# A two-layer graph network: the first mixer's sum of keys by values taken in node order in the head, and the second layer's loop with TensorE, VectorE and ScalarE in a written-out order

## The chip, the cores and the metric

The kernel runs on one core of one Trainium2 chip. A core has TensorE (PE, matrix products and transposes), VectorE (DVE), ScalarE (ACT), GpSimd (POOL, which issues the indirect DMAs here) and SyncE (SP, which issues plain DMAs). The metric is the device time of the whole program in microseconds (us); the profile is one execution recorded by the hardware profiler.

## The reference

There are 3125 nodes with 256 features and 53,125 edges (every random edge both ways, and a loop on each node). Two layers follow one another; each adds message passing, a mixer and a feed-forward part to the residual `x`.

```python
xn = _layernorm(x)
x = x + gnn0(xn, src, dst, edge_weight) + mix0(xn[None])[0]
x = x + ffn0(_layernorm(x)[None])[0]                      # 32 experts, argmax
xn = _layernorm(x)
x = x + gnn1(xn, edge_index, edge_type_64) + mix1(xn[None])[0]
x = x + ffn1(_layernorm(x)[None], edge_index)[0]          # 4 experts, routed by graph attention
```

The first mixer is attention without a softmax. Its `kv` and the norm of each column of `k2` are sums over all nodes, so the order of the nodes does not matter to them:

```python
q, k, v = split(x @ W_qkv + b_qkv)
q2 = (q - mean(q))**2 ; k2 = (k - mean(k))**2
k2 = l2_normalize_over_nodes(k2 / (sum(k2) + eps)) ; q2 = l2_normalize_over_features(q2 / (sum(q2) + eps))
kv = einsum('bnc,bnd->bcd', k2, v)
out = (v + einsum('bnc,bcd->bnd', q2, kv) / sqrt(N)) @ W_out + b_out
```

The second layer's message passing is an attention over the edges of each node, with four heads of 64:

```python
mod_k = K[src] + 0.2 * rel_w[edge_relations][:, None, :]
scores = einsum('ehd,ehd->eh', Q[dst], mod_k) / 8
w = segment_softmax(scores, dst)
msgs = segment_sum(w[:, :, None] * V[src], dst)
out = layernorm(msgs @ Wo + bo + xn) * gamma + beta
```

## The kernel before

Nodes are sorted by degree and put into 25 tiles (`NT`) of 128. Tile `t` has `SLOTS[t]` edge slots a node: 38 in the first tile, 25 in the second, falling to 10 in the last, 444 in all. One indirect DMA of POOL gathers one slot's rows for 128 nodes.

**The head** (`prepare`) counts degrees, sorts the nodes (`ordered`), makes a flag that says whether the fast path holds, and normalizes the 25 tiles of nodes in their given order; SP stores these rows to a table `xtab` in memory. When the head is done, all engines read the flag and branch.

**The front** (`front`) gathers the residual rows in sorted order into `self.xs`, and runs the first mixer (`first_mixer`): for each tile a layernorm (`normed`), a transpose, the products for queries, for keys and values, and for values times output weights (`products`), squares with their statistics (`squares`), and the sum `kvT` of keys by values (`sums`). The generator `counted` (from `sources`), which makes lists of edges, is advanced by one piece at every second tile. Then come a column norm `cn` and a product of `kv` with the output weights, `kvo`. After the mixer follow the first layer's message passing (gathers `g`, added up in `acc` on DVE), the experts, the products of the second layer, and the scatters that build the table `kvtab` of its keys and values.

**The second layer's loop** goes over the tiles. For each tile, `scores` gathers keys and values of up to four slots into one buffer `kv` (14 buffers), adds relation rows `pr`, multiplies by the query `q` and reduces, for each group of four slots; a softmax over the slots follows. `values` scales the value half of each buffer by the softmax weights (ACT, four instructions a slot; DVE takes one slot in eight) and adds them up on PE into `pu` through an identity matrix. `project` makes the output product `pz`. The relation rows come from a one-hot matrix: a transpose of types (`typT`), a product with selectors (`pT`), a comparison on DVE (`ohT`), a product with the relation table (`pr`). For each part of five tiles (the last two parts have three and two), `norms` finishes the second layernorm, and `router_rows` computes the rows of the router table, which POOL scatters to `htab`.

The order of the instructions on each engine is made by a scheduler that follows data and buffers; the routed stage behind the loop is the only one whose order on ACT and DVE is written by hand (`tc.manual_schedule`). The code of the loop asks for the next tile's preparations (`ready`) before the values of this one, and projects the last tile after that:

```python
sc, groups = scores(t, *this)
if t + 1 < NT:
    this = ready(t + 1)
now = t, xq, values(t, xq, sc, groups)
...
project(last[0], last[1], last[2], z[:, i, :], mv[:, i, :])
if last[0] == part[-1]:
    norms(part, z, mv)
    router_rows(part)
```

Behind the loop, the routed stage gathers from `htab` for the 4-expert feed-forward part.

Of the kernel before, what the change touches and what calls it, by code (L numbers as in the profile page):

```python
# [21 lines left out]
P = 128  # L22
N = 3125
D = 256
# [872 lines left out]
class Fast(Net):  # L897
# [32 lines left out]
    def prepare(self, ctx):  # L930
# [11 lines left out]
        flag = keep.tile([1, 1], I32, name="flag")  # L942
        self.ones3 = keep.tile([3, P], BF16, name="ones3")
# [5 lines left out]
        with ExitStack() as ctx:  # L949
# [92 lines left out]
            for t in range(NT):  # L1042
                xn = work.tile([P, D], F32, name="xn")
                self.layernorm(work, self.xs[:, t, :], xn)
                nc.sync.dma_start(self.xtab[t * P:(t + 1) * P, :], xn)
# [280 lines left out]
    def types_by_slot(self, pool, ps, t):  # L1326

        nc = self.nc
        S2 = SLOTS[t] + SLOTS[t] % 2
        pt = ps.tile([S2, P], F32, name="pT")  # L1330
        nc.tensor.transpose(pt, self.typs[t], self.ident)
        typT = pool.tile([S2, P], BF16, name="typT")
        nc.vector.tensor_copy(typT, pt)
        return typT

    def relation_one_hots(self, pool, ps, t, typT, g):

        nc = self.nc
        n = min(8, SLOTS[t] + SLOTS[t] % 2 - g)
        pt = ps.tile([P, 4, P], F32, name="pT")  # L1340
        for i in range(n // 2):
            nc.tensor.matmul(pt[:, i], self.sel[:typT.shape[0], g + 2 * i:g + 2 * i + 2, :].rearrange("s i r -> s (i r)"),
                             typT, start=True, stop=True)
        ohT = pool.tile([P, 4, P], BF16, name="ohT", bufs=3)
        nc.vector.tensor_scalar(ohT[:, :n // 2], pt[:, :n // 2], self.mod, None, op0=OP.is_equal)  # L1345
        return ohT
# [40 lines left out]
    def first_mixer(self, ctx, q2T, nq, kvo, counted):  # L1387
# [5 lines left out]
        w_kv = self.load_kb(big, "w_kv", a["mix0_wkv"])  # L1393
# [3 lines left out]
        b_qkv = self.load_terms(big, big, "b_qkv", a["mix0_b"])  # L1397
# [7 lines left out]
        for c in range(KB):  # L1405
            pw = ps.tile([P, D], F32, name="pqv", bufs=2)
            self.mm_rows(pw, w_vT[:, :, c * P:(c + 1) * P], w_o)
            nc.scalar.copy(w_vo[:, c, :], pw)
# [4 lines left out]
        pw = ps.tile([P, D], F32, name="pqv", bufs=2)  # L1413
# [4 lines left out]
        kvT = ps.tile([P, KB, D], F32, name="kvT")  # L1418
        sqs = big.tile([P, D], F32, name="sqs")
        nc.vector.memset(sqs, 0.0)  # L1420
# [5 lines left out]
        def products(t, xn):  # L1426
            xT = work.tile([P, KB, P], F32, name="xT", bufs=2)
            self.transpose_to(ps, xn, xT)
            pqv = ps.tile([P, 2, D], F32, name="pqv", bufs=2)
            pkv = ps.tile([P, 2 * D], F32, name="pkv", bufs=2)  # L1430
            self.mm_rows(pqv[:, 0], xT, w_q, b_qkv[:, 0:D])
            self.mm_rows(pkv, xT, w_kv, b_qkv[:, D:])
            self.mm_rows(pqv[:, 1], xT, w_vo, b_vo)
            return pqv, pkv

        def squares(t, pqv, pkv):

            pq = pqv[:, 0]
            st = work.tile([P, 2, 6], F32, name="mx_st")
            mv = work.tile([P, 2, 2], F32, name="mx_mv")  # L1440
            nc.vector.bn_stats(st[:, 0, :], pq)
            nc.vector.bn_stats(st[:, 1, :], pkv[:, 0:D])
            for k in range(2):
                nc.vector.bn_aggr(mv[:, k, :], st[:, k, :])
            sd = work.tile([P, 3, 2], F32, name="mx_sd")
            nc.scalar.activation(sd[:, 0, :], mv[:, :, 1], AF.Sqrt, bias=self.eps[:, 1:2],
                                 scale=float(D))
            nc.vector.reciprocal(sd[:, 1, :], sd[:, 0, :])
            nc.vector.scalar_tensor_tensor(sd[:, 2, :], mv[:, :, 0], -1.0, sd[:, 1, :],
                                           op0=OP.mult, op1=OP.mult)  # L1450
            q2 = work.tile([P, D], F32, name="q2")
            k2 = work.tile([P, D], F32, name="k2")
            v = work.tile([P, D], F32, name="v")
            sq = work.tile([P, 2, D], F32, name="sq", bufs=2)
            nc.scalar.activation(q2, pq, AF.Square, bias=sd[:, 2, 0:1], scale=sd[:, 1, 0:1])
            nc.scalar.activation(k2, pkv[:, 0:D], AF.Square, bias=sd[:, 2, 1:2],
                                 scale=sd[:, 1, 1:2])
            nc.scalar.copy(v, pkv[:, D:])
            nc.vector.tensor_add(self.xs[:, t, :], self.xs[:, t, :], pqv[:, 1])
            nc.scalar.activation(sq[:, 0, :], q2, AF.Square, accum_out=nq[:, t:t + 1])  # L1460
            nc.scalar.activation(sq[:, 1, :], k2, AF.Square)
            return q2, k2, v, sq

        def sums(t, q2, k2, v, sq):
            r = rows(t)
            self.transpose_to(ps, q2, q2T[:, :, t * P:(t + 1) * P])
            for k in range(KB):
                nc.tensor.matmul(kvT[:, k, :], v[:r, k * P:(k + 1) * P], k2[:r, :],
                                 start=(t == 0 and k == 0), stop=(t == NT - 1 and k == KB - 1))
            nc.vector.tensor_add(sqs[:r], sqs[:r], sq[:r, 1, :])  # L1470
# [3 lines left out]
        for t in range(NT + 1):  # L1474
            now = None
            if t < NT:
# [3 lines left out]
                now = t, *squares(t, *made)  # L1480
            if last:
                sums(*last)
# [4 lines left out]
        kv = big.tile([P, KB, D], F32, name="kv")  # L1487
        for k in range(KB):
            nc.vector.tensor_copy(kv[:, k, :], kvT[:, k, :])
        cn = work.tile([1, D], F32, name="cn")  # L1490
        csum = ps.tile([1, D], F32, name="pqv", bufs=2)
        nc.tensor.matmul(csum, self.ones[:, 0:1], sqs, start=True, stop=True)
        nc.scalar.activation(cn, csum, AF.Sqrt)
        nc.vector.tensor_scalar_max(cn, cn, 1e-12)
        nc.vector.reciprocal(cn, cn)
        pc = ps.tile([P, KB], F32, name="pqv", bufs=2)
        for k in range(KB):
            nc.tensor.matmul(pc[:, k:k + 1], cn[:, k * P:(k + 1) * P], self.ones[0:1, 0:1],
                             start=True, stop=True)
        rc = work.tile([P, KB], F32, name="rc")  # L1500
        nc.vector.tensor_copy(rc, pc)
        for c in range(KB):
            pw = ps.tile([P, D], F32, name="pqv", bufs=2)
            self.mm_rows(pw, kv[:, :, c * P:(c + 1) * P], w_o)
            nc.vector.tensor_scalar(kvo[:, c, :], pw, rc[:, c:c + 1], None, op0=OP.mult)
# [5 lines left out]
    def front(self, q2T, qT, kvtab, own):  # L1511
# [5 lines left out]
        with ExitStack() as ctx:  # L1517
# [4 lines left out]
            kvo = big.tile([P, KB, D], F32, name="kvo")  # L1522
# [8 lines left out]
            with ExitStack() as mctx:  # L1531
                self.first_mixer(mctx, q2T, nq, kvo, counted)
# [236 lines left out]
    def layers(self):  # L1769
# [7 lines left out]
        with ExitStack() as octx:  # L1777
# [40 lines left out]
            with tc.tile_pool(name="l1_edge", bufs=2, reuse_waits="tile") as ep, \  # L1818
                    tc.tile_pool(name="l1_ps3", bufs=1, space=PSUM, reuse_waits="tile") as ps:
                self.selectors(keep)  # L1820

                def ready(t):

                    xq = ep.tile([P, 2 * D], F32, name="xq", bufs=3)
                    nc.sync.dma_start(xq, own[t * P:(t + 1) * P, :])
                    q = ps.tile([P, D], F32, name="q", bufs=2)
                    nc.scalar.copy(q, xq[:, :D])
                    typT = self.types_by_slot(ep, ps, t)
                    return xq, q, typT, self.relation_one_hots(ep, ps, t, typT, 0)

                def scores(t, xq, q, typT, ohT):
                    S = SLOTS[t]
                    sc = ep.tile([P, S0, 4], F32, name="sc", bufs=3)
                    groups = []
                    for g in range(0, S, 4):
                        n = min(4, S - g)
                        if g % 8 == 0:
                            rr = self.relation_rows(ps, t, ohT, g)
                            if g + 8 < S:
                                ohT = self.relation_one_hots(ep, ps, t, typT, g + 8)  # L1840
                        r0 = g % 8
                        kv = ep.tile([P, 4, 2 * D], F32, name="kv", bufs=14)
# [11 lines left out]
                        nc.vector.tensor_reduce(sc[:, g:g + n, :], k4, axis=AX.X, op=OP.add)  # L1854

# [7 lines left out]
                    nc.scalar.activation(sc[:, :S], sc[:, :S], AF.Exp)  # L1863
                    nc.vector.tensor_reduce(m[:, 0, :], s4, axis=AX.X, op=OP.add)
# [3 lines left out]
                    return sc, groups  # L1868

                def values(t, xq, sc, groups):  # L1870

                    pu = ps.tile([P, D], F32, name="pu", bufs=2)
                    for g, n, kv in groups:
                        for j in range(n):
# [9 lines left out]
                            nc.tensor.matmul(pu, self.ident, v, start=(s == 0), stop=(s == SLOTS[t] - 1))  # L1884
                    return pu

                def project(t, xq, pu, z, mv):
                    u = ep.tile([P, D], F32, name="u")
                    nc.scalar.copy(u, pu)
                    uT = ep.tile([P, KB, P], F32, name="uT")  # L1890
                    self.transpose_to(ps, u, uT)
# [457 lines left out]
```

## Time and profile before

| | us |
|---|---|
| median of 3 runs | 3276.42 (3270.76 to 3286.6) |
| the profiled execution, own time | 3264.12 |
| its span | 3262.3 |
| head, until the flag is made (L1039) | 98 |
| first mixer's loop | 165 to 366 |
| rest of the mixer | 366 to 387 |
| first layer's messages, experts, tables | to 1638 |
| second layer's loop, first gather of `kvtab` to last scatter to `htab` | 1638 to 2601 |
| routed stage | to 3262 |

The profile names a group of instructions by line, engine, operation and tile, with its busy time, the mean time of one, and what ended the idle time of its engine before it ("<-"). An engine's idle time costs something only where the engine is on the path that sets the end. The granted clock (PEclk) is the share of full speed at which TensorE was let run; its mean over the span is 0.761.

### The profile page before, as it was taken

The page shows a single profiled execution, that of the slowest core. Times are in us where ns is not written, and L with a number is a line of the kernel's source. Part 1 is how long each engine was busy: PE and PEld are TensorE (multiplying, and loading weights), DVE is VectorE, ACT ScalarE, POOL GpSimd, SP SyncE. Part 2 cuts the span into 40 slices and gives each one's busy share as a digit, 9 for nine tenths or more (in the row PEclk, how much of TensorE's full clock was granted, in tenths as well). Part 3 has the DMA queues.
Part 4 walks back from the last instruction along what each step waited for, and adds up shares of the span by engine and source line. Part 5 has one row for each costly group of instructions (what it writes and reads, how often), then busy time and mean ns, then how long its engine had stood idle before and what let it go on. Part 6 is the DMA issues. An engine that isn't in the chain of part 4 may idle for free. (4 is left out here: it accounts for less than half of the span.)

```text
span 3262.3 us, 25577 instructions
## 1 busy us (share of the span) xinstructions
PE 1896.8 (58%) x7318; PEld 1140.2 (35%) x7318; DVE 1393.8 (43%) x4055; ACT 872.6 (27%) x2625; POOL 1569.9 (48%) x1675
## 2 busy tenths in 40 slices
PE   0298543556677997415415455665555543867568
PEld 0155222333344554203213343343333322444346
DVE  6487553445444341001237465765655501111026
ACT  0044200111121221001105453655443401312132
POOL 3523466546444216673764664545442074355543
PEclk9899666778788998657757676776776666888789
DMA  4312423223222210000064564545442110000001
GB/s 126 112 60 82 139 83 90 88 83 106 76 84 76 68 42 7 17 4 10 20 194 127 140 179 120 166 127 168 127 127 85 54 32 5 16 7 12 12 7 41
DMA packets 121377, 254.53 MB, mean 78 GB/s; under 512 B 36594, under 2 KB 61926, under 8 KB 120972
## 3 DMA queue, kind: packets, MB, share of 16 engines
q0 software_dynamic: 82656, 196.67, 21.8%
q1 hardware_dynamic: 30316, 47.90, 4.4%
q10 hardware_dynamic: 8256, 8.23, 0.8%
q8 instruction: 61, 1.00, 0.1%
q14 instruction: 88, 0.72, 0.1%
HBM read 228.93 MB, written 23.76 MB: 77 GB/s over the span
## 5 line engine op out<-in xcount | busy, mean ns | idle before, releaser
L1370 POOL DMA_INDIRECT g<-xtab,src x444 | 440.1, 991 | 474.4 <-DVE acc L1376 171.7
L1845 POOL DMA_INDIRECT kv<-kvtab,src x444 | 423.1, 953 | 348.5 <-ACT kv L1882 194.2
L1882 ACT ACTIVATE kv<-kv,sc 128x64 f32<-128x64 f32 x1548 | 380.0, 334 | 78.2 <-issue 48.2
L2056 POOL DMA_INDIRECT ed<-htab,nb x279 | 264.1, 947 | 274.3 <-issue 177.6
L1884 PE MATMUL pu<-kv,ident 128*128 128x256 f32 x888 | 300.6, 469 | 51.2 <-ACT kv L1882 32.1
L1647 PE MATMUL po<-w,h 128*128 128x256 f32 x800 | 230.6, 426 | 131.6 <-ACT h L1633 72.6
L1233 POOL DMA_INDIRECT gl<-gsrc,sidx x256 | 248.9, 972 | 106.9 <-issue 77.3
L2195 PE MATMUL po<-w,h 128*128 128x256 f32 x800 | 208.2, 403 | 87.0 <-issue 86.5
L2183 PE MATMUL ph<-xT,w 128*128 128x512 f32 (+1 forms) x448 | 204.0, 607 | 65.3 <-ACT h L2185 37.4
L1884 PEld LDWEIGHTS pu<-kv,ident 128*128 128x128 f32 x888 | 177.4, 225 | 129.6 <-ACT kv L1882 77.5
L1627 PE MATMUL ph<-xT,w 128*128 128x512 f32 (+1 forms) x448 | 213.7, 594 | 7.3 <-issue 3.6
L1376 DVE SCALAR_TENSOR_TENSOR acc<-g,wt,acc 128x256 f32<-128x256 f32 x419 | 194.8, 477 | 49.0 <-DMA g<-xtab,src 40.5
L1647 PEld LDWEIGHTS po<-w,h 128*128 128x128 f32 x800 | 153.0, 207 | 168.9 <-issue 77.0
L2195 PEld LDWEIGHTS po<-w,h 128*128 128x128 f32 x800 | 155.6, 199 | 136.1 <-issue 118.6
L1633 ACT ACTIVATE h<-ph,b 128x512 f32<-128x512 f32 (+1 forms) x112 | 71.7, 641 | 449.6 <-remote 194.0
L1851 DVE TENSOR_TENSOR kv<-kv,pr 128x1024 f32<-128x1024 f32 (+3 forms) x121 | 133.1, 1123 | 122.9 <-remote 82.3
L1356 PE MATMUL pr<-self.relb,ohT 128*128 128x128 bf16 x687 | 88.5, 289 | 107.3 <-DVE ohT L1345 61.4
L2183 PEld LDWEIGHTS ph<-xT,w 128*128 128x128 f32 x448 | 87.2, 209 | 167.2 <-issue 120.6
L1853 DVE TENSOR_TENSOR kv<-kv,q 128x1024 f32<-128x1024 f32 (+3 forms) x121 | 132.7, 1123 | 0.0
L1854 DVE TENSOR_REDUCE sc<-kv 128x16 f32<-128x1024 f32 (+3 forms) x121 | 132.5, 1121 | 0.1
L2185 ACT ACTIVATE h<-ph,b 128x512 f32<-128x512 f32 (+1 forms) x112 | 68.9, 641 | 229.7 <-PE ph L2183 120.1
L2074 DVE TENSOR_TENSOR ed<-ed 128x288 f32<-128x288 f32 (+12 forms) x16 | 7.5, 466 | 280.7 <-ACT ed L2072 280.7
(437 smaller groups left out, 2985.5 us busy)
## 6 DMA issues: line engine op xcount, KB each, us to landing
dr<-in_gat_dst_row SPq DMA_DIRECT2D x32, 512.0 KB
g<-xtab,src POOLq DMA_INDIRECT x444
kv<-kvtab,src POOLq DMA_INDIRECT x444
own<-xq SPq DMA_DIRECT2D x25, 256.0 KB
xq<-own SPq DMA_DIRECT2D x25, 256.0 KB
ed<-htab,nb POOLq DMA_INDIRECT x279
w<-in_ex_w ACTq DMA_DIRECT2D x2, 2048.0 KB
gl<-gsrc,sidx POOLq DMA_INDIRECT x256
```

The lines of the kernel that those rows point to most:

```text
L1233: ins = nc.gpsimd.indirect_dma_start(out=self.gl[:, :], out_offset=bass.IndirectOffsetOnAxis(ap=self.sidx2[:, c:c + 1], axis=0), in_=self. ...
L1370: nc.gpsimd.indirect_dma_start(out=g[:, s % 4, :], out_offset=None, in_=self.xtab[:, :], in_offset=bass.IndirectOffsetOnAxis(ap=self.srcs[ ...
L1376: nc.vector.scalar_tensor_tensor(acc, g[:, s % 4, :], self.wts[t][:, s:s + 1], acc, op0=OP.mult, op1=OP.add)
L1627: nc.tensor.matmul(ph[:, :n], w1[:, k, mc], xT[:, k, :n], start=(k == 0), stop=False)
L1647: nc.tensor.matmul(pos[j // 2][:, j % 2], this[:, j * P:(j + 1) * P], w2[:, m, :], start=False, stop=(m == M - 1 and (j % 2 == 1 or j == w ...
L1845: nc.gpsimd.indirect_dma_start(out=kv[:, j, :], out_offset=None, in_=kvtab[:, :], in_offset=bass.IndirectOffsetOnAxis(ap=self.srcs[t][:, g ...
L1851: nc.vector.tensor_tensor(k4, k4, rr[:, r0:r0 + n].unsqueeze(2).to_broadcast([P, n, 4, HD]), op=OP.add)
L1882: nc.scalar.activation(v[:, h * HD:(h + 1) * HD], v[:, h * HD:(h + 1) * HD], AF.Copy, scale=sc[:, s, h:h + 1])
L1884: nc.tensor.matmul(pu, self.ident, v, start=(s == 0), stop=(s == SLOTS[t] - 1))
L2056: nc.gpsimd.indirect_dma_start(out=ed[:, s, :], out_offset=None, in_=self.htab[:, :], in_offset=bass.IndirectOffsetOnAxis(ap=self.nbrs[t][ ...
L2183: nc.tensor.matmul(ph[:, :w], w1[:, e, k, m * P:(m + 1) * P], xT[:, :len(ts), k, :], start=(k == 0), stop=(k == KB - 1))
L2195: nc.tensor.matmul(po[:, i], hs[i][:, m, j * P:(j + 1) * P], w2[:, e0 + i, m, :], start=False, stop=(i == 1 and m == M - 1))
```

## The change

In the head, each tile of nodes, once normalized, is also transposed and multiplied by the keys' and values' weights; statistics and squares follow, and the sum of keys by values and the sum of squared keys build up in PSUM over the 25 tiles. The column norm is made there. The results (`kvs`, `rc`) are kept for the front. The first mixer keeps only the queries and the values times output weights. In the second layer's loop, the order on ACT, DVE and PE is written out by hand; POOL's and SP's is left to the scheduler. Projections, norms and router rows are generators of which `behind` takes a step twice in every group of slots; projections go ahead of norms. Queries are held in PSUM for two tiles, relation rows are asked for a pair of groups ahead with a PSUM tile (`pS`) of their own, and the sum of a group's values on PE is written one group behind its scaling.

```diff
@@ prepare @@
-            for t in range(NT):
-                xn = work.tile([P, D], F32, name="xn")
-                self.layernorm(work, self.xs[:, t, :], xn)
-                nc.sync.dma_start(self.xtab[t * P:(t + 1) * P, :], xn)
+            w_kv = self.load_kb(one, "w_kv", a["mix0_wkv"])
+            b_kv = self.load_terms(one, one, "b_kv", a["mix0_b"][D:])
+            kvT = ps.tile([P, KB, D], F32, name="kvT")
+            csum = ps.tile([1, D], F32, name="csum")
+            def keys(t, xn):
+                xT = work.tile([P, KB, P], F32, name="xT", bufs=2)
+                self.transpose_to(ps, xn, xT)
+                pkv = ps.tile([P, 2 * D], F32, name="pkv", bufs=2)
+                self.mm_rows(pkv, xT, w_kv, b_kv)
...
+                nc.vector.bn_stats(st, pkv[:, 0:D])
+                nc.vector.bn_aggr(mv, st)
+                nc.scalar.activation(sd[:, 0:1], mv[:, 1:2], AF.Sqrt, bias=self.eps[:, 1:2], scale=float(D))
+                nc.vector.reciprocal(sd[:, 1:2], sd[:, 0:1])
+                nc.vector.scalar_tensor_tensor(sd[:, 2:3], mv[:, 0:1], -1.0, sd[:, 1:2], op0=OP.mult, op1=OP.mult)
...
+                nc.scalar.activation(k2, pkv[:, 0:D], AF.Square, bias=sd[:, 2:3], scale=sd[:, 1:2])
+                nc.scalar.copy(v, pkv[:, D:])
+                nc.scalar.activation(sq, k2, AF.Square)
+                return k2, v, sq
+            def sums(t, k2, v, sq):
+                r = rows(t)
+                for k in range(KB):
+                    nc.tensor.matmul(kvT[:, k, :], v[:r, k * P:(k + 1) * P], k2[:r, :],
+                                     start=(t == 0 and k == 0), stop=(t == NT - 1 and k == KB - 1))
+                nc.tensor.matmul(csum, self.ones[:r, 0:1], sq[:r, :], start=(t == 0), stop=(t == NT - 1))
+            last = None
+            for t in range(NT + 1):
+                now = None
+                if t < NT:
+                    xn = work.tile([P, D], F32, name="xn", bufs=20)
+                    self.layernorm(work, self.xs[:, t, :], xn)
+                    nc.sync.dma_start(self.xtab[t * P:(t + 1) * P, :], xn)
+                    now = t, *keys(t, xn)
+                if last:
+                    sums(*last)
+                last = now
+            nc.scalar.copy(self.kvs, kvT)
+            cn = one.tile([1, D], F32, name="cn")
+            nc.scalar.activation(cn, csum, AF.Sqrt)
+            nc.vector.tensor_scalar_max(cn, cn, 1e-12)
+            nc.vector.reciprocal(cn, cn)
...
+            nc.vector.tensor_copy(self.rc, pc)
@@ first_mixer @@
-            pqv = ps.tile([P, 2, D], F32, name="pqv", bufs=2)
-            pkv = ps.tile([P, 2 * D], F32, name="pkv", bufs=2)
-            self.mm_rows(pqv[:, 0], xT, w_q, b_qkv[:, 0:D])
-            self.mm_rows(pkv, xT, w_kv, b_qkv[:, D:])
+            pqv = ps.tile([P, 2, D], F32, name="pqv", bufs=3)
+            self.mm_rows(pqv[:, 0], xT, w_q, b_q)
             self.mm_rows(pqv[:, 1], xT, w_vo, b_vo)
...
-            nc.vector.bn_stats(st[:, 1, :], pkv[:, 0:D])
...
-            nc.scalar.activation(k2, pkv[:, 0:D], AF.Square, bias=sd[:, 2, 1:2],
-                                 scale=sd[:, 1, 1:2])
-            nc.scalar.copy(v, pkv[:, D:])
...
-            nc.scalar.activation(sq[:, 1, :], k2, AF.Square)
...
-            nc.vector.tensor_add(sqs[:r], sqs[:r], sq[:r, 1, :])
...
-        csum = ps.tile([1, D], F32, name="pqv", bufs=2)
-        nc.tensor.matmul(csum, self.ones[:, 0:1], sqs, start=True, stop=True)
-        nc.scalar.activation(cn, csum, AF.Sqrt)
...
+            nc.vector.tensor_scalar(self.kvs[:, c, :], pws[c], self.rc[:, c:c + 1], None, op0=OP.mult)
@@ the second layer's loop @@
+                ctx3.enter_context(tc.manual_schedule(
+                    engines={mybir.EngineType.Activation, mybir.EngineType.DVE, mybir.EngineType.PE}))
+                def values(t, sc, groups, pu):
+                    was = []
+                    for g, n, kv in groups + [(0, 0, None)]:
+                        for s, v in was:
+                            nc.tensor.matmul(pu, self.ident, v, start=(s == 0), stop=(s == SLOTS[t] - 1))
+                        was = []
...
+                def behind(n):
+                    while n and (todo[0] or todo[1]):
+                        q = todo[0] if todo[0] and free[0] else todo[1]
+                        r = next(q[0], todo)
...
+                    for i in range(n):
+                        g = 4 * i
+                        if g % 8 == 0:
+                            if g + 8 < SLOTS[t]:
+                                rel = rows_of(t, g + 8)
+                            elif t + 1 < NT:
+                                rel = rows_of(t + 1, 0)
+                            else:
+                                rel = iter(())
+                            next(rel, None)
+                        if i == 1 and t + 1 < NT:
+                            xq1 = query(t + 1)
+                            nc.scalar.copy(qs[:, (t + 1) % 2], xq1[:, :D])
+                            types = self.types_by_slot(ep, ps, t + 1, typT[(t + 1) % 2])
+                            next(types)
+                        next(steps)
+                        behind(1)
+                        if g % 8 == 0:
+                            next(rel, None)
+                        for _ in types:
+                            pass
+                        if i == 0 and vals is not None:
+                            for _ in vals[5]:
+                                pass
+                        for _ in range(-(-left // (n - i))):
+                            next(vals[4])
+                            left -= 1
+                        if g % 8 == 4 or i == n - 1:
+                            next(rel, None)
+                        behind(1)
+                    next(steps)
+                    if vals is not None:
+                        projected(vals[0], vals[1], vals[3])
```

`steps` is `scores` as a generator with one step a group; `rows_of` is `relations_by_slot`, whose three steps are the selector product, the comparison, and the relation rows. `norms` is the old `norms` and `router_rows` in one generator.

## The prediction

> **What bounds the kernel now.** I read the page first, for the engines' shares and for the slices. The chain of waits on it covers only the last stage, so it says nothing of the two stages that the change touches, and I went on to a table of windows, then to the waits of POOL, DVE and PE inside the second layer's loop, and to the groups of the first mixer.
>
> ```profile
> PE 1896.8 (58%) x7318; PEld 1140.2 (35%) x7318; DVE 1393.8 (43%) x4055; ACT 872.6 (27%) x2625; POOL 1569.9 (48%) x1675
> ```
>
> No engine is full over the span, so each stage has its own limit. The windows (us; the columns are length, PE, PEld, DVE, ACT and POOL busy, the granted TensorE clock, DMA share, GB/s):
>
> ```profile
> 60.00:100.00 40.00, 6.67 (x35) 3.39 (x34) 29.39 (x83) 0.82 (x4) 4.78 (x5) 1.00 0.10 33
> 165.00:366.00 201.00, 179.05 (x840) 101.58 (x838) 156.28 (x694) 87.93 (x267) 65.98 (x65) 0.93 0.24 73
> 366.00:390.00 24.00, 6.65 (x30) 4.31 (x30) 10.43 (x27) 1.35 (x4) 7.57 (x8) 0.52 0.28 79
> 1737.00:1980.00 243.00, 138.84 (x573) 89.13 (x569) 135.16 (x204) 133.18 (x519) 157.34 (x166) 0.72 0.60 169
> 1980.00:2260.00 280.00, 168.39 (x747) 110.62 (x748) 181.78 (x290) 142.99 (x567) 136.72 (x144) 0.71 0.47 136
> 2260.00:2500.00 240.00, 132.18 (x552) 87.01 (x552) 134.19 (x241) 108.29 (x417) 105.96 (x112) 0.68 0.45 132
> ```
>
> The head (up to 98 us, where the flag is made) is a chain on DVE beside an idle PE. The first mixer, 165 to 366 us, is bound by PE: 179 of 201 us, with DVE second at 156. In the second layer's loop, 1638 to 2600 us, nothing is above 65% after 1980. What it waits for (us in total, times, longest):
>
> ```profile
> POOL kv L1845 <- ACT kv L1882: 194.2, 23, 28.0
> POOL htab L1940 <- issue: 149.5, 24, 62.4
> ...
> PE pT L1342 <- DVE typT L1333: 117.3, 13, 39.9
> PE pr L1356 <- DVE ohT L1345: 61.4, 21, 13.5
> ...
> DVE kv L1851 <- remote: 82.3, 9, 26.0
> ```
>
> POOL stands twice: its gathers lack free buffers, and its scatters into the router table wait for the norms. PE waits for small things of DVE, and DVE for PE: engines waiting on one another's order, not on work. Between 2366 and 2500 a tile takes 33 us in which no engine is busy for 60% of it. The whole loop is 962 us for 25 tiles, 38.5 a tile.
>
> **The change, part by part.** The sum is made against the profiled execution: 3264.1 us, of which 3262.3 is span. It ran 12 us under the median of 3276.4, so a result against the median has that much play.
>
> *Head.* Per node tile PE gains a transpose, the keys' and values' products, the sum of keys by values, and the sum of squares. From the mixer's groups:
>
> ```profile
> L926 PE MATMUL pkv<-w_kv,xT 128*128 128x512 f32 x96 | 54.8, 679 | 0.0
> L926 PE MATMUL pqv<-w_q,xT 128*128 128x256 f32 x96 | 29.2, 429 | 18.0 <-ACT xT L127 17.9
> L1468 PE MATMUL kvT<-k,v 128*128 128x256 f32 (+1 forms) x100 | 26.5, 389 | 0.0
> L1441 DVE BATCH_NORM_STATS2 mx_st<-pqv 128x6 f32<-128x256 f32 x25 | 10.8, 430 | 9.5 <-PE pqv L927 5.3 <-remote 3.9 <-issue 0.2
> ```
>
> A group there is four passes per tile, so pkv is 54.8/24 = 2.3 us a tile, its bias 0.4, kvT 1.06, two transposes 0.6, the sum of squares at a pass of 256 about 0.5: 4.7 us with overlap, 25 x 4.7 = 117 us of PE. DVE gains 0.43 + 0.17 (bn_aggr) + 0.16 (reciprocal) + 0.15 = 0.9 us a tile, ACT about 1.9. In the compiled order 15 tiles' statistics stand before the flag on DVE and 10 behind it. The 14 us that this puts before the flag fill partly the 10.6 us that DVE idles from 60 to 100; I take the flag at 106. Then ten tiles at PE's 4.7 us, and 6 us for the column norm (square root, reciprocal, two small matmuls, copy): the head ends at 159 in place of 100: +59. Below: PE starts at 14 us and never waits, 14 + 117 + 6 = 137: +38. Above: the last ten at the clock of 0.74 that the stretch 100 to 165 shows, +75. The weights' two loads (512 KB and a row) go out on ACT's queue in the first microseconds; DVE's eleventh instruction waits for that row, and everything of DVE behind it with it, some 3 us which are in the 106. SP's 25 stores of normalized rows go out with each tile as before, ahead of the flag or behind it. No POOL work of the later stages covers the longer head: all engines branch on the flag only after the head, so the first gather of node rows moves with it.
>
> *First mixer.* PE loses 54.8 + 9.8 + 26.5 = 91 us of 179, DVE 25 x (0.43 + 0.17 + 0.42 for the added squares) = 25 of 156, ACT 35 of 88. PE's cover over DVE is gone and DVE is next: 131 us busy, which at 90 to 95% filling is 138 to 146 us, plus the start of the pipeline, so 153 for 201: -48. At the end the copies of the sum and the column norm go: about -10 of the 24 us. Together -58, against +59: nothing. Bounds are -30 (the loop waits for what else DVE has, the counting) and -75. The front stage behind it (390 to 1638) is planned anew; its POOL order is nearly unchanged, so I take 0 +- 30.
>
> *Loop, start.* A 28 us stall of POOL at 1737, when the first tile's buffers fill, ends: the first tile's values go two groups a step.
>
> *Loop, norms.* Before, projection, norms and router rows of five tiles run in one burst in which POOL sits in front of scatters (four blocks of 10.8 to 15.7 us and as much again behind them for buffers, about 100 us, then 62 and 27 at the end). After, they are spread over the steps; in POOL's order the scatters of tiles 0 to 4 stand behind the sixteenth gather of tile 10, while DVE has finished those rows at the end of tile 8, and 14 buffers reach just from tile 8 to there. So POOL hardly stands. The scatters of the last ten tiles remain at the end, 20 to 40 us.
>
> *Loop, a tile.* Worked out by the fixed order with the durations above. The first two groups: selectors and transposes 1.3 us of PE, then the previous tile's first group scaled by ACT (15 x 0.245 us, the busy time of the scaling group, 380.0 us, over its 1548 instructions) and added by PE (4 x 0.45), projection 3.5 to 3.9, relation rows 1.3: about 16.5 us, in which DVE stands 4.5 to 7 us at the third group for the relation rows that are late. Each further group costs ACT's 16 x 0.245 = 3.9, with waits 4.4 us. A tile has 121/25 = 4.84 groups: 16.5 + 2.84 x 4.4 + 1 = 30 us, and 27 for the later ones. POOL's own rate is 1.25 us an issue (0.95 busy and 0.30 between), 26 us an average tile. Sum: first two tiles 98, seven large tiles 228, sixteen later ones 430, end 40: 796 us. The waits called "remote" (82 + 48 + 47 us on DVE) and the handing over between engines are not in this; no row of before shows them in the new order, so they lie between 0 and 177. I take a quarter, 45, as most of them stand in the bursts that go: 841, -121 against 962.
>
> Two rules bear on this. The clock: the trace grants 0.68 to 0.72 in this loop, and the same shape takes 403 ns in a dense stage (po) against 586 here (pz). The Trainium skill, "TensorE: Matmul & The Clock Gate", in "What's actually happening", says that TensorE falls to half rate after an idle window of about 3.4 us; the fixed order has PE wait some 8 us for ACT at each tile's start. By the trace PE's work is 22 us a tile, hidden under 30. By the rule it is 22 x 0.7 / 0.5 = 31, and PE becomes the bound: 98 + 23 x 31 + 40 + 45 = 896, -66. The measured clock already has pauses of 10 to 40 us in it, so I keep it; the end goes into the range. And "ScalarE: Activation LUTs", "What ACT_TABLE_LOAD costs", puts 2.66 us on each switch of table; square roots scattered between exponentials would cost up to 24 x 2.7 = 64 us. The trace shows no such row, but the compiled order has 9 loads in the loop where before had 11: nothing.
>
> Sum: 3264 + 59 - 58 + 0 - 121 = 3144.
>
> **The rivals.**
>
> *A, the likeliest (0.46):* as above, loop 780 to 890 us: 3080 to 3210.
>
> *B, POOL becomes the bound (0.11):* all stalls go, the loop falls to 485 issues x 1.25 = 606 plus 40 at the end, 650 to 750. For it: 1737 to 1980 ran 166 issues in 243 us. Against: the relation rows come late by my own count. 2960 to 3060.
>
> *C, the gain is half taken back (0.17):* the head costs +59, the mixer loop stays where it was because counting and sums fill DVE (-30), and POOL still stands at its scatters, whose place in its queue is not among the fixed orders, so that of its 100 us half remains: loop -70. 3264 + 29 - 70 = 3223. That the merged norms do not reach the scatters in time is also the form in which the change would not do what it says.
>
> *D, slower (0.20):* lock-step. The relation rows stand on PE behind value matmuls that wait for ACT's scaling; if DVE stands for them not once a tile but at every later pair of groups (1.42 a tile), each us of stall costs 1.42 x 25 = 36 us. It decides from 121/36 = 3.4 us a pair. At the 5.6 us of my middle stall: +199 against -121, 3342. For it: a fixed order cannot take another tile's ready work, and DVE already waits 15 us for pr. Against: rows are asked for one pair ahead, and the pu matmuls lag one group.
>
> *No change (0.06):* C with the half-rate clock.
>
> **How the numbers follow.** About 0.5%, 16 us, is what a measurement can tell from no change. Faster is A, B and C: 0.74; within it 0.06; slower 0.20. The range leaves out B's lower half and D's upper part: 3020 to 3310. A's own range is 3080 to 3210.
>
> **What would show it.** The flag near 106 and the first gather of node rows near 160; the mixer loop about 150 us with DVE above 85% busy and PE about 60%; POOL's wait at the scatter line inside the loop under 50 us and no 28 us stall early; 27 to 30 us a late tile; DVE's wait for pr grown to some 100 to 170 us in all. If the head grew by over 80 us, or the loop kept 33 us a late tile, or DVE's wait for pr passed 300 us, the prediction is wrong in that step.

## The result, and the profile after

The changed kernel takes 3379.5 us (median of 4; 3367.9 to 3405.7) beside 3281.5 for the kernel before (median of 4; 3270.8 to 3288.5): 1.032 times as long, interval 1.028 to 1.036. Forecast were 3144, range 3020 to 3310.

The page of the changed kernel, engines over the span (the profiled execution took 3405.7 us, the longest of the four; the one before took 3264.1, 17 us under this median, so the two profiles differ by 142 us where the medians differ by 98):

```profile
PE 1969.6 (58%) x7416; PEld 1173.6 (34%) x7416; DVE 1421.4 (42%) x4082; ACT 880.2 (26%) x2674; POOL 1571.3 (46%) x1675
```

The work is nearly the same. The table of windows, columns as in the prediction, cut at the changed kernel's own stages:

```profile
60.00:108.00 48.00, 42.27 (x149) 18.24 (x149) 39.31 (x156) 18.85 (x60) 4.73 (x5) 0.93 0.15 47
108.00:181.00 73.00, 49.78 (x138) 20.72 (x137) 11.55 (x43) 18.12 (x53) 24.64 (x26) 0.84 0.19 55
240.00:345.00 105.00, 90.56 (x474) 56.16 (x472) 78.33 (x398) 48.39 (x144) 0.00 (x0) 0.80 0.12 42
...
1818.00:2060.00 242.00, 124.01 (x533) 80.05 (x533) 126.18 (x171) 115.43 (x467) 140.01 (x147) 0.67 0.52 147
2060.00:2340.00 280.00, 151.72 (x651) 102.29 (x651) 172.78 (x274) 128.53 (x512) 123.86 (x130) 0.67 0.45 129
2340.00:2618.00 278.00, 157.92 (x679) 105.39 (x679) 175.37 (x278) 133.53 (x534) 136.34 (x143) 0.69 0.48 136
```

Read them with three sets of starts, by tile. First the flag: DVE makes it at 106.6 us as forecast, SP and POOL read it at once, but ACT, PE and DVE read it only behind the keys of the last ten tiles.

```profile
L1100 POOLq TENSOR_LOAD <-flag x1: 501/501/501, 106.7 to 106.7; - x1
L1100 DVEq TENSOR_LOAD <-flag x1: 546/546/546, 180.5 to 180.5; - x1
```

Then the gathers (the two last times of a line are its first and its last start): messages in the kernel before, then in the changed one messages, keys and values of the loop, and the scatters of the router table.

```profile
L1370 POOL DMA_INDIRECT g<-xtab,src x444: 940/946/3127, 135.6 to 1155.8; - x148
L1430 POOL DMA_INDIRECT g<-xtab,src x444: 942/949/3396, 189.6 to 1220.0; - x148
L1865 POOL DMA_INDIRECT kv<-kvtab,src x444: 942/949/2913, 1719.4 to 2618.7; - x148
L1990 POOL DMA_INDIRECT htab<-hx,pid x25: 957/962/1206, 2186.4 to 2742.3; - x25
```

Before, the last two went from 1638.6 to 2484.7, and to 2600.7. So the loop starts 81 us later, although the mixer ends 35 us earlier (352 in place of 387); the loop itself takes 1023 us in place of 962; the routed stage behind it is the same (661 us in both). What POOL waits for beside the mixer, and what DVE waits for in the loop:

```profile
POOL g L1430 <- DVE src L1337: 143.3, 1, 143.3
L1434 DVE TENSOR_SCALAR acc<-g,wt x25: 335/347/484, 356.6 to 1218.0; 128x256 f32<-128x256 f32 x25
```

The first line names a copy of edge lists on DVE, but this is only the instruction that ended last: the 16 gathers before it had filled the four buffers of `g`, and DVE starts the first sum that frees them at 356.6 us, behind the mixer (second line).

```profile
DVE kv L1873 <- ACT q L2062: 109.2, 19, 5.8
DVE kv L1871 <- remote: 94.6, 10, 19.5
DVE kv L1871 <- PE pr L1416: 53.5, 25, 4.6
DVE kv L1873 <- ACT kv L1906: 44.6, 4, 20.3
DVE z L1927 <- PE pz L1925: 33.2, 15, 9.8
```

Neither stands in the prediction: 143 us in which POOL gathers no message while the mixer runs, and a wait of the multiplication by the query for a copy on ACT.

### The profile page after: what moved, and what is told of

Its sections match the earlier page's. It is cut to its first block, busy times and chain, and to the rows that moved or that the text cites. A ratio compares the mean times of both kernels' runs of the same rounds, so it can differ in the third digit from the quotient of the medians.

```text
span 3403.8 us, 25700 instructions
## 1 busy us (share of the span) xinstructions
PE 1969.6 (58%) x7416; PEld 1173.6 (34%) x7416; DVE 1421.4 (42%) x4082; ACT 880.2 (26%) x2674; POOL 1571.3 (46%) x1675
## 5 line engine op out<-in xcount | busy, mean ns | idle before, releaser
L1671 PE MATMUL po<-w,h 128*128 128x256 f32 x800 | 242.9, 444 | 168.4 <-ACT h L1657 88.1
L1896 PEld LDWEIGHTS pu<-kv,ident 128*128 128x128 f32 x888 | 201.5, 247 | 261.5 <-ACT kv L1906 180.9
L2304 PE MATMUL po<-w,h 128*128 128x256 f32 x800 | 210.4, 407 | 83.2 <-issue 82.9
L1671 PEld LDWEIGHTS po<-w,h 128*128 128x128 f32 x800 | 161.0, 217 | 208.6 <-issue 98.4
L2304 PEld LDWEIGHTS po<-w,h 128*128 128x128 f32 x800 | 156.7, 201 | 131.9 <-issue 114.0
L1416 PE MATMUL pr<-self.relb,ohT 128*128 128x128 bf16 x687 | 64.8, 258 | 138.8 <-DVE ohT L1403 65.9
```

The costliest lines, as they stand in the source:

```text
L1671: nc.tensor.matmul(pos[j // 2][:, j % 2], this[:, j * P:(j + 1) * P], w2[:, m, :], start=False, stop=(m == M - 1 and (j % 2 == 1 or j == w ...
L2304: nc.tensor.matmul(po[:, i], hs[i][:, m, j * P:(j + 1) * P], w2[:, e0 + i, m, :], start=False, stop=(i == 1 and m == M - 1))
```

## The experiments

The chips differ: where the experiments ran, the kernel before took 2617 us on some chips and about 3320 on others (3281 in the first measurement), so each ratio is to the kernel before on the same chip.

**1. The two halves alone, and together.** `e1_head` has the new head and mixer with the old loop, `e2_loop` the old head and mixer with the new loop, `a_after` is the changed kernel, `b_before` the one before.

> Only the first half of the change: keys, values and their sum in the head, the mixer without them; the second layer's loop as before. Theory 1 (the head ends 80 us later, the mixer's end only 35 us earlier, and the message gathers that lay beside the mixer now stand behind it): slower than before by 60 to 85 us. Theory 2 (the whole loss is lock-step in the loop, the head is repaid by the mixer): within 15 us of before.

> Only the second half: the second layer's loop with its orders written out, head and mixer as before. Theory 1: slower by 30 to 60 us, as the loop of the changed kernel was 60 us longer in the profile. Theory 2: slower by about 100 us.

> The changed kernel itself, beside the parts of it. If the two halves add up on this chip (87 us for the head, 96 us for the loop), it is slower than before by 165 to 195 us, 6 to 7.5%. If the halves share a cause, or hide one another, it is slower by 80 to 130 us, near the 3.2% of the first measurement.

> The kernel before, for its profile on the chip of the experiments. Expected from the parts: the first gather of the key and value table near 1378 us, the loop from there to the last scatter near 772 us; both short of the first profile by the waits that it names issue and remote, with the same order of work.

| kernel | us | ratio to before | first gather of the loop | loop |
|---|---|---|---|---|
| `b_before` | 2617.6 | | 1379.5 | 776 |
| `e1_head` | 2703.1 | 1.034 (1.032 to 1.036) | 1465.0 | 772 |
| `e2_loop` | 2712.9 | 1.037 (1.035 to 1.039) | 1377.5 | 873 |
| `a_after` | 2803.2 | 1.071 (1.069 to 1.073) | 1468.1 | 873 |

The halves are two causes, and they add: 87 and 96 us make 183, and 186 was measured. Theory 2 falls, as the head is not repaid; but both halves lost more than theory 1 had said (60 to 85 and 30 to 60 us), and the loop alone lost 96, near the 100 that theory 2 had for it. That the ratio is 1.071 here and 1.032 in the first measurement goes with waits that only the profiles of the slower chips show at this size; see the last section.

**2. Messages beside the mixer.** In the traces, 66 of DVE's 419 additions of messages start before the mixer's last statistics in the kernel before, and none in the changed one. The messages come behind the mixer in the program. That the scheduler filled DVE's gaps with them while PE set the mixer's pace, and put them off once it counted DVE as busy, is my reading of this; no run shows how it chose. `e4_msgs` writes those of the first three tiles into the mixer's loop of `e1_head`, four slots at each step (the `yield` stands in the sum over a tile's slots):

```diff
+            if s % 4 == 3:
+                yield
...
             last = now
+            next(early, None)
             if t % 2:
                 next(counted)
```

> As the head-only kernel, but the gathers and sums of the first three tiles' messages (86 slots) are written into the mixer's loop, four slots a node tile. If the messages that were pushed behind the mixer are what the front lost: 50 to 90 us faster than the head-only kernel, so from 30 us faster to 20 us slower than before. If the front is bound by PE or the experts and the messages hide there anyway: within 15 us of the head-only kernel.

2654.0 us, 1.0145 (1.013 to 1.016): 49 of the 87 us come back, just under the 50 to 90 expected, and 37 us are still missing where at most 20 were. The message lines, first of `e1_head`, then of `e4_msgs`:

```profile
L1424 POOL DMA_INDIRECT g<-xtab,src x444: 941/946/4388, 167.5 to 1042.0; - x148
```

```profile
L1428 POOL DMA_INDIRECT g<-xtab,src x444: 940/946/2000, 167.9 to 993.8; - x148
```

The first gather starts at the same time and the last 48 us earlier, and the loop's first gather moves by 50, from 1465.0 to 1415.4. So the gathers and their sums lie on the path that sets the time of the front, and are not hidden by PE or the experts.

**3. A head that costs little.** What remains is 37 us. `e6_one_tile` makes the keys of the last tile only, and leaves the other 24 out of the sum:

```diff
-                    now = t, *keys(t, xn)
+                    if t == NT - 1:
+                        now = t, *keys(t, xn)
```

> As the kernel with messages beside the mixer, but the head makes keys, values and their sum for the last tile only, so the sum over the other 24 tiles is left out. It shows what the shorter mixer is worth with a head that costs nothing. If the head's longer end is what is left of the loss: 40 to 60 us faster than the kernel with messages, 0 to 20 us faster than before. If the front stage is paced by something else: the gain stays under 25 us.

2628.8 us, 1.004 (1.003 to 1.006; the profiled execution 2617.8): 25 us faster than `e4_msgs`, at the edge of the second case. Its head is not quite free, as the flag comes at 105.4 us for 98.0 before. But even with the keys' work gone from the mixer and nearly all of it not put anywhere else, the kernel is not faster than before. The windows of the mixer's loop, and the products of the queries in it, bear on why; first the kernel before, then `e6_one_tile`:

```profile
165.00:316.00 151.00, 144.57 (x736) 85.08 (x736) 135.45 (x586) 75.02 (x227) 64.34 (x62) 0.99 0.28 87
```

```profile
170.00:340.00 170.00, 124.68 (x567) 74.47 (x564) 129.58 (x587) 60.42 (x172) 89.39 (x87) 0.69 0.33 99
```

```profile
L926 PE MATMUL pqv<-w_q,xT 128*128 128x256 f32 x100 | 28.2, 404 | 3.2 <-ACT xT L127 3.1
L926 PE MATMUL pqv<-w_q,xT 128*128 128x256 f32 x100 | 43.2, 572 | 9.2 <-ACT xT L127 9.0
```

DVE does 130 us in place of 135 (more messages, fewer statistics). In the kernel before it was 90% full already, beside PE at 96%, so the loss of 169 matmuls on PE frees little. And PE's busy time falls by only 20 us: its granted clock goes from 0.99 to 0.69, and a matmul of the same shape takes 572 ns in place of 404. In `e6_one_tile` neither engine is full (73% and 76%), so the order still costs something there; other numbers of messages in the loop were not tried.

**4. The query's copy.** DVE's chain in one late tile of the changed kernel:

```profile
2486.35 1.21 DVE L1871 TENSOR_TENSOR kv<-kv,pr 128x1024 f32<-128x1024 f32 x1
2493.36 1.22 DVE L1873 TENSOR_TENSOR kv<-kv,q 128x1024 f32<-128x1024 f32 x1 [5.79 <-ACT q L2062]
```

Columns are start, duration and instruction, with the idle time before it and who ended it. The copy is of the next tile's query, into the other half of the same PSUM tile; this tile's query has long been there. The multiplication, written behind that copy, waits for it all the same, and on ACT the copy stands behind 28 scalings (6.8 us):

```profile
2486.01 6.79 ACT L1906 ACTIVATE kv<-kv,sc 128x64 f32<-128x64 f32 x28 [4.50 <-DVE sc L1888]
2492.70 0.35 ACT L1920 COPY uT<-pT 128x256 f32<-128x256 f32 x1
2492.96 0.37 ACT L2062 COPY q<-xq 128x256 f32<-128x256 f32 x1
```

`e3_copy_first` puts the copy one group earlier in the loop of `e2_loop`:

```diff
-                        if i == 1 and t + 1 < NT:
+                        if i == 0 and t + 1 < NT:
                             xq1 = query(t + 1)
                             nc.scalar.copy(qs[:, (t + 1) % 2], xq1[:, :D])
+                        if i == 1 and t + 1 < NT:
                             types = self.types_by_slot(ep, ps, t + 1, typT[(t + 1) % 2])
```

> As the loop-only kernel, but the copy of the next tile's query into PSUM stands one group earlier in ACT's order, ahead of the scaling of the last tile's first groups. Theory A (VectorE's second multiplication of each tile waits for that copy, 5.8 us, as both queries lie in one PSUM tile): the wait of 109 us for q goes, and the kernel is 60 to 130 us faster than the loop-only one. Theory B (the relation rows are late anyway, so the wait moves to them): 0 to 25 us faster than the loop-only one, and the wait of VectorE for pr grows from 54 us to over 130.

2710.7 us, 1.036 (1.034 to 1.039): 2 us. The wait is gone and the time is not. DVE's waits in its loop, of `e2_loop`:

```profile
DVE kv L1855 <- ACT q L2044: 132.5, 23, 5.8
DVE kv L1853 <- PE pr L1362: 67.5, 31, 4.7
...
DVE z L1909 <- PE pz L1907: 39.9, 22, 11.3
```

and of `e3_copy_first`:

```profile
DVE z L1909 <- PE pz L1907: 145.8, 24, 9.8
DVE kv L1853 <- PE pr L1362: 68.7, 29, 5.6
```

Theory B was right that the wait moves, and wrong on where: not to the relation rows (68 us in both) but to the projection's sum.

**5. Values last.** All three waits have one place: the copy, the projection's `uT` and so `pz`, and the relation rows stand on ACT or PE behind a tile's first scalings and their sum. `e5_values_last` puts the relation rows and the step of `behind` (the projection's, or one of norms where no projection is open) ahead of them, on the loop of `e3_copy_first`:

```diff
-                        for _ in range(-(-left // (n - i))):
-                            next(vals[4])
-                            left -= 1
                         if g % 8 == 4 or i == n - 1:
                             next(rel, None)
                         behind(1)
+                        for _ in range(-(-left // (n - i))):
+                            next(vals[4])
+                            left -= 1
```

> As the kernel with the query's copy first; in each group of slots the step of the projection and the relation rows now stand ahead of the scaling and summing of the last tile's values, on ACT, PE and DVE. If the loop is slow because what VectorE needs next (the projection's sum, 6.9 us of waiting a tile, and the relation rows, 2 to 3.5 us) is queued on ACT and PE behind 28 scalings: 60 to 110 us faster than the copy-first kernel, the loop near 780 us. If the waits only move again (ACT's scaling late, buffers held longer): within 25 us of it.

2565.3 us, 0.980 (0.978 to 0.982): 145 us faster than `e3_copy_first`, more than the 60 to 110 expected, and 2% faster than the kernel before. Its waits and windows:

```profile
DVE kv L1853 <- DMA kv<-kvtab,src: 64.1, 9, 42.2
DVE z L1909 <- PE pz L1907: 30.6, 5, 9.3
...
DVE kv L1853 <- PE pr L1362: 11.9, 17, 2.8
```

```profile
1377.00:2008.00 631.00, 422.48 (x1961) 270.30 (x1961) 530.75 (x794) 379.28 (x1520) 452.18 (x475) 0.77 0.68 197
```

DVE is now 84% full up to the last gathers, where `e2_loop` has 69% (517 of 748 us); the loop takes 724 us in place of 873 and of 776 before.

**6. Its two halves.** `f3` and `f5` are the two ends again, `f7_projection` moves only the projection's step, `f8_relations` only the relation rows; all four ran on one chip. `e7_projection` and `e8_relations` are the same two kernels on a slower chip.

> The copy-first loop again, as the slow end of the four. Where the kernel before takes 2617 us: 3.4 to 3.9% slower than it. Where it takes about 3300 us: 1 to 2.5% slower, as waits that all kernels have there cover part of it.

> The values-last loop again, as the fast end. Where the kernel before takes 2617 us: 1.8 to 2.2% faster than it. Where it takes about 3300 us: 0.8 to 2% faster.

> Only the projection's step ahead of the values. If the projection's wait is the main part: at least 55% of the way from copy-first to values-last. If each half leaves the other's wait to fill the gap: under 50% of the way, with VectorE's wait for pr above 70 us.

> Only the relation rows ahead of the values. If the projection's wait is the main part: under 40% of the way from copy-first to values-last, VectorE's wait for pz above 110 us. If the relation rows are: over 55% of the way.

> As the copy-first kernel, with only the projection's step moved ahead of the values; the relation rows stay behind them. If the projection's wait (6.9 us a tile) was the main part of the 146 us: 60 to 110 us faster than copy-first. If the relation rows were: under 40 us faster, as VectorE's wait for pr then grows past 100 us.

> The other half: only the relation rows moved ahead of the values. If the projection's wait was the main part: 20 to 60 us faster than copy-first, its wait for pz staying near 146 us. If the relation rows were: over 80 us faster.

| kernel | us | ratio | wait for pz | wait for pr |
|---|---|---|---|---|
| `f3_copy_first` | 2715.0 | 1.036 | 145 | 71 |
| `f7_projection` | 2632.8 | 1.005 | 32 | 106 |
| `f8_relations` | 2661.8 | 1.016 | 151 | 6 |
| `f5_values_last` | 2564.3 | 0.979 | 31 | 11 |

The projection's step is worth 82 of the 151 us, the relation rows 53, both together 15 more than their sum. So the projection is the larger part, though at 54.5% of the way it falls short of the 55 I had set, and with it alone the wait for `pr` does grow, to 106 us. On the chip where the kernel before takes 3322 us the order is the same: `e7_projection` 0.996 (0.994 to 0.998), `e8_relations` 1.006 (1.004 to 1.008), 39 us apart where `f7` and `f8` are 29. The copy-first loop did not run there, so what each is worth there can't be read.

**7. The old place of the copy, and the whole change mended.** `e9_copy_old` (again `f9_copy_old`) is values-last with the copy back at the second group. `e10_mended` (again `f10_mended`) has the head, mixer and messages of `e4_msgs` and the loop of `e5_values_last`.

> As the kernel with the values last, but the query's copy back in its old place, one group later. If the copy was late only because it stood behind the scalings: within 15 us of values-last, as 12 or 16 scalings now stand between, not 28 with the step of the projection behind them. If the one PSUM tile for both queries costs a wait of its own each tile: 50 to 130 us slower than values-last.

> Both halves of the change, each mended: keys and their sum in the head, messages of three tiles beside the mixer, and the loop with the values last. If the parts add: 37 us slower in the front and 52 us faster in the loop, so 5 to 25 us faster than before and 30 to 45 us slower than the loop with values last alone.

> Values last, query's copy in its old place. If the wait for the copy has a price of its own: 40 to 90 us slower than values-last where the kernel before takes 2617 us (19 waits of about 5.8 us were seen on the other chip, 114 us in all, part of which would be idle anyway). If it only takes the place of other waits, as it did before the values stood last: within 15 us.

> Both halves, each mended. If the parts add where the kernel before takes 2617 us: +37 for the front and -54 for the loop, so 10 to 25 us faster than before (0.99 to 0.996), and 30 to 45 us slower than values-last with the old head. If the head gains there as it did on the slower chip: 40 us or more faster than before.

All four fell on slower chips (3322 and 3318 us before), so the expected differences to `e5_values_last` can't be read, and the mended change was not measured on a fast one. `e9_copy_old` has 0.991 and 0.989, with 114 us of waits for the copy in its loop; `e10_mended` has 0.981 and 0.982 (0.976 to 0.988), 3259.1 and 3267.0 us. The mended change gains about 1.9% on chips like the one where the change lost 3.2%, 51 to 63 us and so more than the 5 to 25 first expected. Its head costs less there: in the profiles the loop's first gather comes at 1693 beside 1687 for `e9_copy_old` (1697 and 1672 in the second pair), where `e4_msgs` was 36 us behind the kernel before; and its loop is 24 and 42 us shorter than that of `e9_copy_old`, which is what the copy's place would be worth there. With one execution each, and the front different too, that is a reading, not a measurement.

## Why the prediction was wrong

- **Head, +59.** The flag came at 106.6 (forecast 106). The end came at 180.5 for 159; on the faster chips it came at 158.7. The step was right in its work; the 22 us are gaps of PE, ACT and DVE, the longest 15 us on DVE, where no gap in this stretch is over 4.2 us on the faster chip. That the first gather of node rows moves with the head's end was wrong: POOL read the flag at 106.7 and had done these gathers by 141. What did move was the message gathers, from 135.6 to 189.6.
- **Mixer and front, -58 and 0 +- 30.** From the head's end to the mixer's end it was 171 us in place of 287, more than forecast, because the messages were no longer there; the front behind it then took 1367 us (352 to 1719) in place of 1252. The failing step is the zero: "its POOL order is nearly unchanged". POOL's order of gathers nearly was; DVE's order was not, and POOL's gathers wait for DVE's sums. With head and mixer together the term was +1 and measured +81 in the profiles, +87 on the faster chip. I had counted the messages' sums inside the 131 us of DVE in the mixer, and they had left it. Also, a removed 91 us of PE was not worth 48 once messages were back in the loop: DVE, at 90% on the faster chip (78% in the trace of the forecast), stood just behind PE, and the lower clock took back part of it (experiment 3).
- **Loop, -121.** It was +61 in the profiles and +96 on the faster chip. Two terms failed. The first is the tile: the seven large tiles were put at 228 us and the sixteen later ones at 430; from softmax to softmax they took 319 and 516, and 255 and 476 on the faster chip (`a_after`), where the first two tiles (97 us for 98) and the end (46 for 40) came as forecast. I had given DVE one wait of 4.5 to 7 us a tile, for relation rows. It had the query's copy (154 us with those that the trace puts down to the scaling), and behind that, covered by it, up to 6.9 us for the projection (`e3_copy_first`: 6.9 in 12 of 25 tiles), which my chain of the first two groups had put on PE and ACT without asking which DVE instruction comes next and needs it. The second is the 45 us for waits called "remote", on the ground that most of them go. Judged by the two chips they did not go: the changed loop takes 150 us more on the slower chip (1023 and 873), the old one 186 more (962 and 776). Without such waits, my own 796 us would have been no gain, as the old loop takes 776 there.
- **Loop, norms.** Taking the scatters and norms out of the way worked in part. The bursts inside the loop went, but the longest stall early in the loop stayed (34 us for 28), and the scatters' wait fell only from 149.5 to 116 us (`POOL htab L1990 <- issue: 116.0, 18, 97.5`). Of this, 97.5 lie behind the last gather, where DVE still has the last tiles to do; from the last softmax to the last scatter it is 44 us, near the 40 of the sum.
- **Signs.** The mixer's loop was to show DVE above 85% and PE near 60%; from 240 to 345 us PE has 86% and DVE 75%, as the messages are not there, so its shorter time is no hit of the reasoning. The head grew by 80 us, at the bound that I had set for it. A late tile took 32 us for 27 to 30. DVE's wait for the relation rows was 53.5 us, below the 100 to 170 forecast.
- **Rivals.** C named the failing half of the front (a head that is not repaid) with the wrong reason, and gave it 0.17. D named lock-step and gave 0.20, with relation rows as its place; in the loop with the copy first the rows are a third of it (53 of 151 us), the projection the larger part. A and B fell. (POOL's 485 issues at 1.25 us make 24 us a tile and not 26; nothing rests on it.) The chances were wrong where 0.46 went to a sum whose two largest terms were found by adding up one engine's work at a time.
- **Clock.** The loop's granted clock was 0.67 to 0.69, as the trace had said and above the half rate that I had weighed against it.
- **Tables.** That the trace shows no row for a switch of table was a misreading. The loop has 11 loads of 1.28 us in the kernel before and 9 in the changed one, and the next instruction can start 0.01 us behind a load. That is under 12 us in all, so the term of nothing stands.

## What to carry to other kernels

An order that is written out is only as good as the answer to one question at each step: what does the fullest engine need next, and what stands ahead of that on the engine that makes it. Work that nobody waits for soon (here the scalings of an older tile) goes last in each step. And before work is taken from the engine that sets a stage's pace, look at the second engine's fill, and at what a scheduler had put into its gaps: that work is what comes back behind the stage.

## What the runs showed of the hardware

The same program, with the same 0.95 us for an indirect DMA, takes 2617 us on some chips and 3280 to 3320 on others. The slower profiles have waits named "remote" and "issue" of up to 78 us on ACT, DVE and PE. The faster ones have none named "remote", and none named "issue" of over 7 us on these engines. These are of the kernel before on the first chip:

```profile
ACT h L1633 <- remote: 194.0, 15, 47.0
DVE xs L1587 <- remote: 89.8, 7, 26.4
```

The routed stage, which no kernel here changed, shows it plainly: 661 us against 461. What these waits are, no run shows. That they cover part of the stalls that an order makes would fit 1.032 for the changed kernel there and 1.071 here, but it is not shown. A forecast from one chip's profile holds for the waits of that chip.

Two halves of one PSUM tile count as one in waits here: in `e2_loop`, 23 of 24 tiles waited about 5.8 us for a write to the half that they did not read. Whether the chip or the way the program sets its waits makes it so, no run shows; two tiles of their own were not tried.
